# Setup of a two-layer graph kernel on one core: the score weights come in first, by column halves, and VectorE's setup work is reordered

## The chip, the cores and the metric

The kernel runs on one core of a Trainium2 chip. The metric is device time in microseconds (us) of one execution. Before the change three runs took 2207.53 us in the median (2207.39 to 2207.76).

A core has TensorE (PE, matrix products; PEld is its loading of weights), VectorE (DVE), ScalarE (ACT), GpSimd (POOL) and SyncE (SP), which here only issues transfers. Each takes its own instructions in the order in which they were built, and they wait for one another through semaphores. ACT and POOL issue transfers too. Transfers (DMAs) of all three run on the same 16 DMA engines: those of SP and ACT in two hardware queues, those of POOL in a software queue.

## The reference

128 graphs of 128 nodes with 512 features go through two layers. Cut to what matters:

```python
h = relu(layernorm(x))                         # layer 0
Xw = h @ Wv + bv
e  = leaky_relu((Xw @ aw[:d])[:, None, :] + (Xw @ aw[d:])[:, :, None] + ab, 0.2)
T  = adj * exp(e);  T = T / (T.sum(-1) + 1e-12)
x  = x + relu(h @ Wk[0] + T @ h @ Wk[1] + T @ T @ h @ Wk[2] + bk.sum(0))

h = relu(layernorm(x))                         # layer 1
q, k = split(h @ Wqk)
w  = mask / sqrt(512) * (q * (adj @ (k * mask))).sum(-1)
x  = x + softmax(w)[:, :, None] * (h @ Wv1)
```

All is fp32. `Wqk` is 512 x 1024 (2 MB), each `Wk[k]` and `Wv` is 512 x 512 (1 MB).

## The kernel before

**Algebra.** `Xw` is never formed: `Wv @ aw[:d]` and `Wv @ aw[d:]` are two columns (`attention_columns`, L252) that are put beside `Wk[2]` in the operand `r2` (`w` in the profile), so that one product of `h` gives `h Wk[2]` and both attention terms. `Wk[1]` and `Wk[0]` stand side by side in `r10` (`r` in the profile). For layer 1, the product of the two halves of `Wqk` is formed once (`score_matrix`, L316, the score matrix `M`, kept in `rl`), since `q . (adj k)` is a bilinear form of `h`.

**Products.** A product of `h` with 512 x 512 weights is done by `strassen` (L412): seven half-size products 1, 5, 6, 2, 7, 3, 4 in PSUM banks a, b, c, e, with sums of the left operand (`left_sums`, `sx`) and of the right one (`combine_steps`, L196: four subtractions on DVE, kept in `t2` for `r2` and in `t10` for `r10`; `t10` is `t` in the profile). The right operand of product 5 is the first subtraction, of 6 the second, of 7 the third, of 4 the fourth; products 1, 2 and 3 take plain blocks. `y2` (L487) is the product with `r2`, `y10` (L622) that with `r10`.

**Loops.** Graphs are taken in pairs. Layer 0 is a loop over 64 pairs (L809): `y10(p)`, `inner`, `outer`, `y2(p+2)`, `norm2`. Layer 1 is a loop over 32 groups of two pairs (L1157). All of this is unchanged.

**Setup (L762 to 805)** runs before the loop, and is what the change touches. Nothing may be reordered inside a chain that the code gives: `ordered` chains all products on PE, `behind("wk", ...)`, `behind("wq", ...)` and `tc.issue_after` put an instruction after a named one; within that, a planner chose the order of each engine when the program was built. The order on PE is:

1. `warm` and `warm_whole` (L226 to 237): products of ones that nobody reads, 7 small (128 columns), one of 512 columns, and later one of 512 and four small ones between the transposes;
2. 32 transposes of `Wqk` (`weights_transposed`, L301), one 128-row chunk after the other; ACT and DVE copy them out into `wqt` and `wkt`;
3. 8 transposes of the first pair's `h` and one of the node mask;
4. `score_matrix(f)` for f = 0 to 3, four products of 512 columns each;
5. `y2(0)`, whose first product needs `r2` with its attention columns, then `spread_columns(0)` and `y10(0)`, each of whose products needs `r10` or its combinations. The four products of 1 column between products 7 and 3 of `y2(0)` (`attention_constant`, L273) make a constant from `bv`, `aw` and `ab`, which DVE prepares in `constant_columns` (L266).

**Transfers.** SP issues `x` of pair 0, the four chunks of `Wqk` (512 KB each, rows of 4 KB), `x` of pair 1, then of each of `Wv` (`t` in the profile, it lies in the space of `t10`), `Wk[2]`, `Wk[1]` and `Wk[0]` the first two of four pieces. A piece (`rows`, L170) is 256 KB and goes to 32 partitions. POOL issues the other two pieces of each, after a small copy (`gate`, L178) that waits for the third chunk of `Wqk`; between those of `Wk[2]` and of `Wk[1]` it issues the three tiny loads `bvc`, `awc`, `ab_bc`, and after all of them the block-wise `adj` of pairs 0 and 1 (`agb`, L111).

Of the kernel before, what the change touches and what calls it, by code (L numbers as in the profile page):

```python
# [16 lines left out]
def kernel(  # L17
# [25 lines left out]
    nc = tc.nc  # L43
    B, N, D = x.shape
    K = wk.shape[0]
    P = 128
    DC = D // P
# [35 lines left out]
    def behind(what, op, *args, **how):  # L83

        with tc.issue_after(done[what]):
            return op(*args, **how)  # L86

    def ordered(op, *args, **how):

        with tc.issue_after(done["mm"]):  # L90
            done["mm"] = op(*args, **how).ins  # L91

    def bcast(ap, offset, n):

        return bass.AP(tensor=ap.tensor, offset=ap.offset + offset, ap=[[0, P], [1, n]])
# [45 lines left out]
    awc = setup.tile([P, 2, DC], FP, name="awc")  # L141
    bvc = setup.tile([P, DC], FP, name="bvc")

    load_x(0)
    for c in range(DC):
        nc.sync.dma_start(wqk_sb[:, c], wqk[c * P:(c + 1) * P])  # L146
    load_x(1)
    def blocks32(ap, offset, times, n):
        return bass.AP(tensor=ap.tensor, offset=ap.offset + offset, ap=[[0, times], [S32, n], [1, S32]])

# [19 lines left out]
    def rows(dst, w, chunks=range(DC), queue=nc.sync):  # L170

        for c in chunks:
            queue.dma_start(dst[c * S32:(c + 1) * S32],
                              w[c * P:(c + 1) * P].rearrange("(f a) o -> a f o", a=S32))


    gate = setup.tile([P, 1], FP, name="gate")
    done["gate"] = nc.gpsimd.tensor_copy(gate, wqk_sb[:, 2, :1]).ins  # L178
    weights0 = [(wv0_sb, wv0), (r2[:, :, 1:1 + D], wk[2])] + [(r10[:, :, k], wk[1 - k]) for k in range(2)]
    with tc.issue_after(done["gate"]):  # L180
        for dst, w in weights0[:2]:
            rows(dst, w, range(HC, DC), nc.gpsimd)
        nc.gpsimd.dma_start(bvc, bv0.rearrange("(p c) -> p c", c=DC))
        nc.gpsimd.dma_start(awc, aw.rearrange("(a p c) o -> p a (c o)", a=2, c=DC))
        nc.gpsimd.dma_start(ab_bc, bcast(ab, 0, 1))
        for dst, w in weights0[2:]:
            rows(dst, w, range(HC, DC), nc.gpsimd)
    for dst, w in weights0:
        rows(dst, w, range(HC))
    load_x(2)  # L190

# [34 lines left out]
    def warm_whole(bank):  # L226

        with tc.issue_after(done["mm"]):
            done["mm"] = nc.tensor.matmul(bank.rearrange("p (k n) -> p k n", n=P), ones,
                                          ones[:, None, :].to_broadcast([P, D // P, P]), start=True, stop=True).ins  # L230

    def warm(times, bank, start=True):

        for _ in range(times):
            with tc.issue_after(done["mm"]) if "mm" in done else ExitStack():
                done["mm"] = nc.tensor.matmul(bank[:, :P], ones, ones, start=start, stop=True,
                                              skip_group_check=True).ins
# [48 lines left out]
    def bias_columns():  # L286

        n = HD // S32
        v = bkt[:, 0, :2 * n]
        behind("wk", nc.vector.transpose, bkt.rearrange("p s j -> p (s j)"), bkj.rearrange("p s r -> p (s r)"))  # L290
        nc.vector.tensor_add(v, v, bkt[:, 0, 2 * n:])
        nc.vector.tensor_add(v, v, bkt[:, 1, :2 * n])
        done["wk"] = nc.vector.tensor_sub(v[:, n:], v[:, n:], v[:, :n]).ins

    def bias():

        n = HD // S32
        for i, to in enumerate((bias_a, bias_e)):
            behind("wk", over_partitions, to[:, 1], bkt[:, 0, i * n:(i + 1) * n], n)

    def weights_transposed(chunks):  # L301

        banks = [a2, e2, a1, b1, c1, e1]
        for c in chunks:
            for a in range(2):
                bank = banks[(c * 2 + a) % len(banks)]
                pt = bank.rearrange("p (o i) -> p o i", o=DC)
                for o in range(DC):
                    at = a * D + o * P
                    ordered(nc.tensor.transpose, pt[:, o, :], wqk_sb[:, c, at:at + P], ident)  # L310
                if a:
                    done["wk"] = behind("wq" if c == HC else "wk", nc.scalar.copy if c == HC else nc.vector.tensor_copy, wkt[:, :, c * P:(c + 1) * P], pt).ins
                else:
                    done["wq"] = behind("wq", nc.scalar.copy, wqt[:, :, :, c, :], pt.rearrange("p o (f a) -> p o f a", f=Q)).ins

    def score_matrix(f):  # L316

        bank = set1[f]
        for o in range(DC):
            ordered(nc.tensor.matmul, bank, wqt[:, o, f].rearrange("p c a -> p (c a)"), wkt[:, o],  # L320
                    start=(o == 0), stop=(o == DC - 1))
        done["m"] = done["mm"]
        nc.scalar.copy(rl[:, f, 0], bank)
# [68 lines left out]
    def transposed_by_pe(h, dst, banks):  # L392

        for j in range(G):
            pt = banks[j].rearrange("p (f n) -> p f n", f=Q)
            for f in range(Q):
                ordered(nc.tensor.transpose, pt[:, f, :], h[:, j, f * P:(f + 1) * P], ident)
            (nc.vector.tensor_copy if j else nc.scalar.copy)(dst[:, j], pt)

    def left_sums(hT):  # L400

# [357 lines left out]
                lambda: dve(nc.vector.tensor_sub, s[:, 3], b[0, 1], s[:, 1])]  # L759


    warm(7, e2)  # L762
    warm_whole(b2)
    done["warm"] = done["mm"]
    h0_rs = statistics(xg[0])
    done["wk"], done["wq"] = done["rs"], done["ln"]
    weights_transposed(range(1))
    h0 = behind("wq", norm_relu, xg[0], True, h0_rs)
    done["wq"] = done["h"]
    attention_vector_columns()  # L770
    attention_vector(0)
    warm_whole(c2)
    weights_transposed(range(1, 2))
    attention_vector(1)
    bias_columns()
    warm(2, b2, False)
    weights_transposed(range(2, 3))
    warm(2, b2, False)
    weights_transposed(range(3, 4))
    hT0 = lefts.tile([P, G, DC, N], FP, name="x")  # L780
    transposed_by_pe(h0, hT0, (a1, b1))
    masks()
    bias()
    rs1 = behind("wk", statistics, xg[1], "wq")
    LEFT[0] = left_sums(hT0)
    behind("left", attention_columns)
    for p in range(2):
        load_adj(p)
    for f in range(Q):
        score_matrix(f)  # L790
    behind("wq", norm0, 1, rs1)
    with tc.issue_after(done["u"]):
        right2 = combine(halves(r2, W2), [t2[:, i] for i in range(4)])
    constant_columns()
    with tc.issue_after(done["right"]):
        right10 = combine(halves(r10, HD), pairs(t10))
    with tc.issue_after(done["right"]), tc.issue_after(done["m"]):
        y2(0, {7: attention_constant})
        seed_a()
        seed_e()  # L800
        spread_columns(0)
        attention(0)
    with tc.issue_after(done["hv"]):
        load_x(3)
        load_adj(2)

    RS0 = {}

    for p in range(NP):  # L809
        weights, weights_end = [], None  # L810
# [622 lines left out]
```

## Time and profile before

| what | value |
|---|---|
| median of three runs | 2207.53 us |
| profiled execution, its own time | 2207.71 us |
| its span | 2205.9 us |
| PE busy | 2197.3 us (100% of the span) |
| DVE, ACT, POOL busy | 1699.8, 1233.0, 782.6 us |
| first product of `y2(0)` starts | 28.27 us |
| product 5 of `y10(0)` starts | 37.12 us |

The span is the time between the first and the last instruction of the core; 1.8 us of the execution's own time lie around it. PE is busy from 1.1 us on to the end, with 8.6 us of gaps in all, so a change in the setup is worth what it moves the work that PE can't skip. In the answers of the trace each line has a start and a length in us, then the engine, the source line, and what is written from what; in brackets stands the idle time before it and what ended it. A line number is often that of a helper, so the names of the tiles tell more.

### The profile page before, as it was taken

What the parts mean: (1) busy time and instruction counts of PE and PEld (TensorE: products, weight loads), DVE (VectorE), ACT (ScalarE), POOL (GpSimd) and SP (SyncE); (2) the same over time, 40 slices, a digit from 0 to 9 for tenths busy, and PEclk for the clock granted to TensorE, in tenths of its full rate; (3) what the DMA queues carried; (4) which work ended last, traced back from release to release, by engine and by line L of the source; (5) the groups of instructions that cost most, each with busy time, mean ns of one, the idle gap of its engine ahead of it and who ended that gap; (6) DMA issues with size and microseconds to landing.
All of it is one profiled execution on the core that took longest, in us unless ns stands there. A gap on an engine that the chain in (4) does not pass through costs nothing.

```text
span 2205.9 us, 29564 instructions
## 1 busy us (share of the span) xinstructions
PE 2197.3 (100%) x8127; PEld 1536.1 (70%) x8127; DVE 1699.8 (77%) x4544; ACT 1233.0 (56%) x2854; POOL 782.6 (35%) x957
## 2 busy tenths in 40 slices
PE   9999999999999999999999999999999999999998
PEld 6666666665666666566666666688788878887886
DVE  6778788777878877777877777588777777777777
ACT  4555555555555455555545554456666666666665
POOL 3222222222222222222222222255545554555454
PEclk9999999999999999999999999999999999999999
DMA  7788788887878888887878887867888788787877
GB/s 212 204 226 241 221 237 241 234 245 226 247 223 244 234 239 234 225 245 225 243 222 239 232 232 207 285 180 220 234 226 228 214 236 224 231 212 230 233 212 182
DMA packets 431874, 503.14 MB, mean 228 GB/s; under 512 B 102113, under 2 KB 280289, under 8 KB 427741
## 3 DMA queue, kind: packets, MB, share of 16 engines
q1 hardware_dynamic: 379544, 374.67, 56.1%
q0 software_dynamic: 51744, 126.05, 23.2%
q8 instruction: 65, 1.06, 0.2%
q14 instruction: 101, 0.82, 0.1%
q10 hardware_dynamic: 420, 0.54, 0.1%
HBM read 287.17 MB, written 213.94 MB: 227 GB/s over the span
## 4 chain that ended last, share of the span: by engine, by line
PE 98%; DMA 1%; DVE 1%; issue 0%; SPq 0%; DVEq 0%; POOL 0%
PE a L91 29%; PE c L91 26%; PE b L91 26%; PE e L91 17%; DMA t<-in_L_gnn_Wv_dram 0%; DMA tl<-in_L_gnn_Wqk_dram 0%; DVE junk L258 0%; DVE c L720 0%; DVE h L720 0%; DVE junk L720 0%; SPq L146 0%; DVEq L1429 0%; DVE x L389 0%; PE a L194 0%; SPq L101 0%
## 5 line engine op out<-in xcount | busy, mean ns | idle before, releaser
L720 POOL TENSOR_TENSOR c<-s,c 128x512 f32<-128x512 f32 (+1 forms) x186 | 201.2, 1095 | 252.3 <-DVE s L720 247.2
L475 POOL DMA_DIRECT2D fd<-fw x124 | 78.8, 639 | 492.8 <-DVE fw L463 458.5
L111 POOL DMA_DIRECT2D agb<-in_adj_dram x256 | 149.9, 592 | 260.2 <-DVE aT L86 235.5
L91 PE MATMUL a<-r,x 128*128 128x512 f32 x512 | 240.7, 592 | 0.0
L91 PE MATMUL b<-rw,in 128*128 128x256 f32 x884 | 212.0, 379 | 0.0
L91 PEld LDWEIGHTS b<-rw,in 128*128 128x128 f32 x884 | 168.0, 190 | 23.3 <-issue 0.5
L91 PEld LDWEIGHTS a<-r,x 128*128 128x128 f32 x512 | 97.1, 190 | 95.0 <-issue 91.3
L86 ACT COPY s<-c 128x257 f32<-128x257 f32 (+1 forms) x128 | 61.6, 481 | 171.4 <-PE c L91 171.4
L86 ACT COPY b<-a 128x257 f32<-128x257 f32 (+1 forms) x128 | 59.4, 464 | 167.7 <-PE a L91 165.2
L720 POOL TENSOR_TENSOR c<-c 128x1024 f32<-128x1024 f32 x61 | 144.2, 2363 | 10.9 <-DVE c L720 10.4
L91 PE MATMUL a<-w,x 128*128 128x257 f32 x512 | 132.0, 380 | 1.2 <-DVE w L86 1.1
L91 PE MATMUL b<-w,sx 128*128 128x257 f32 x512 | 132.1, 380 | 0.1
L463 DVE STREAM_TRANSPOSE fw<-hv 128x256 f32<-128x256 f32 x248 | 88.3, 414 | 52.1 <-DMA hv<-h2d 51.7
L91 PE MATMUL c<-t,sx 128*128 128x512 f32 x256 | 120.3, 592 | 0.0
L91 PE MATMUL e<-t,sx 128*128 128x512 f32 x256 | 120.3, 592 | 0.0
L91 PE MATMUL c<-t,x 128*128 128x512 f32 x256 | 120.3, 592 | 0.0
L91 PE MATMUL b<-t,sx 128*128 128x512 f32 x256 | 120.3, 592 | 0.0
L91 PE MATMUL b<-r,sx 128*128 128x512 f32 x256 | 120.3, 592 | 0.0
L720 DVE SCALAR_TENSOR_TENSOR junk<-agg,wscale,c 128x512 f32<-128x512 f32 x126 | 96.2, 763 | 30.0 <-POOL c L720 24.8
L720 ACT ACTIVATE c<-c,wcol 128x512 f32<-128x512 f32 x124 | 86.3, 720 | 55.7 <-DVE wcol L720 55.7
L86 ACT COPY c<-b 128x257 f32<-128x257 f32 (+1 forms) x128 | 59.4, 464 | 98.9 <-PE b L91 98.9
L91 PEld LDWEIGHTS a<-w,x 128*128 128x128 f32 x512 | 97.1, 190 | 15.9 <-DVE w L86 1.9
(282 smaller groups left out, 5318.3 us busy)
## 6 DMA issues: line engine op xcount, KB each, us to landing
fd<-fw POOLq DMA_DIRECT2D x93, 512.0 KB, 4.8
xg<-in_x_dram SPq DMA_DIRECT2D x64, 512.0 KB, 7.0
x1d<-x SPq DMA_DIRECT2D x64, 512.0 KB, 5.6
h2d<-h SPq DMA_DIRECT2D x64, 512.0 KB, 3.0
hd<-h SPq DMA_DIRECT2D x63, 512.0 KB, 3.1
hv<-hd SPq DMA_DIRECT2D x252, 128.0 KB, 3.9
hv<-h2d SPq DMA_DIRECT2D x248, 128.0 KB, 4.4
h<-h2d SPq DMA_DIRECT2D x62, 512.0 KB, 7.7
```

What stands on the lines that cost most here:

```text
L86: return op(*args, **how)
L91: done["mm"] = op(*args, **how).ins
L111: nc.gpsimd.dma_start(agb[p][c * S32:(c + 1) * S32].rearrange("p g q i -> p (g q) i"), v[c])
L463: done["c12"] = nc.vector.transpose(blocks[:, k, j].rearrange("p f (n b) -> p f n b", n=Q), hv[:, j].rearrange("p n (k f a) -> p k f n a", ...
L475: done["fd"] = nc.gpsimd.dma_start(FD[q].rearrange("p o j k n -> p o (j k n)")[:, slots], FW[0].rearrange("p o j k n -> p o (j k n)")[:, s ...
L720: done[engine] = op(*args, **how).ins
```

## The change

Six edits, all in the setup:

- `Wqk` is loaded in eight pieces of 256 KB (rows of 1 KB) in place of four of 512 KB: first the column half 0 of all chunks, then half 1. SP issues chunks 0 and 2, ACT chunks 1 and 3. `x` of pair 0 follows in SP's queue; it was first.
- All four pieces of `Wv` and of `Wk[2]` go into SP's queue, with `x` of pair 1 between the two. POOL's `gate` waits for `Wv`; after it POOL issues its two pieces of `Wk[1]` and of `Wk[0]`, then `bvc`, `awc`, `ab_bc`.
- The dummy products shrink to one small one and two of 512 columns, all at the start.
- `weights_transposed` takes a row half and a column half; `score_matrix` takes a column half, and each of the four sums is made of two parts, with the transposes of the next halves between them.
- On DVE, `attention_columns` come ahead of `left_sums`; the statistics of pair 1, the biases and the constant's columns move behind the combinations of `r2`; the four combinations of `r10`, which stood ahead of `y2(0)`'s additions, move behind them and into `attention(0)`.
- On ACT, both halves of pair 0's transposed `h` are copied (DVE copied one); the normalisation of pair 1 moves from ahead of `y2(0)` to behind its product 7.

The core of the diff:

```diff
+    for oh in range(2):
+        for ch in range(2):
+            for c in range(HC):
+                at = ch * HC + c
+                (nc.scalar if c else nc.sync).dma_start(
+                    wqk_sb[:, at].rearrange("p (a o) -> p a o", a=2)[:, :, oh * HD:(oh + 1) * HD],
+                    wqk[at * P:(at + 1) * P].rearrange("p (a o) -> p a o", a=2)[:, :, oh * HD:(oh + 1) * HD])
     load_x(0)
-    for c in range(DC):
-        nc.sync.dma_start(wqk_sb[:, c], wqk[c * P:(c + 1) * P])
-    load_x(1)
...
-    done["gate"] = nc.gpsimd.tensor_copy(gate, wqk_sb[:, 2, :1]).ins
     weights0 = [(wv0_sb, wv0), (r2[:, :, 1:1 + D], wk[2])] + [(r10[:, :, k], wk[1 - k]) for k in range(2)]
+    for dst, w in weights0[:2]:
+        rows(dst, w)
+        if dst is wv0_sb:
+            load_x(1)
+    done["gate"] = nc.gpsimd.tensor_copy(gate, wv0_sb[:, DC - 1, :1]).ins
     with tc.issue_after(done["gate"]):
-        for dst, w in weights0[:2]:
+        for dst, w in weights0[2:]:
             rows(dst, w, range(HC, DC), nc.gpsimd)
         nc.gpsimd.dma_start(bvc, bv0.rearrange("(p c) -> p c", c=DC))
         nc.gpsimd.dma_start(awc, aw.rearrange("(a p c) o -> p a (c o)", a=2, c=DC))
-        nc.gpsimd.dma_start(ab_bc, bcast(ab, 0, 1))
-        for dst, w in weights0[2:]:
-            rows(dst, w, range(HC, DC), nc.gpsimd)
-    for dst, w in weights0:
+        done["loads"] = nc.gpsimd.dma_start(ab_bc, bcast(ab, 0, 1)).ins
+    for dst, w in weights0[2:]:
         rows(dst, w, range(HC))
     load_x(2)
...
-    warm(7, e2)
+    warm(1, e2)
     warm_whole(b2)
-    done["warm"] = done["mm"]
-    h0_rs = statistics(xg[0])
...
+    warm_whole(c2)
+    done["warm"] = done["wk"] = done["wq"] = done["mm"]
+    weights_transposed(0, 0, (a2, e2))
+    weights_transposed(1, 0, (c1, e1))
+    attention_vector_columns()
+    attention_vector(0)
+    weights_transposed(0, 1, (a2, e2))
+    attention_vector(1)
+    score_matrix(0, 0)
+    masks()
+    score_matrix(1, 0)
+    h0_rs = behind("wk", statistics, xg[0], "wq")
+    behind("aggr", bias_columns)
+    weights_transposed(1, 1, (a2, e2))
+    score_matrix(2, 0)
+    score_matrix(3, 0)
     h0 = behind("wq", norm_relu, xg[0], True, h0_rs)
...
+    score_matrix(0, 1)
+    transposed_by_pe(h0, hT0, (a2, e2))
+    behind("wk", behind, "rs", attention_columns)
+    LEFT[0] = behind("u", left_sums, hT0)
+    for f in range(1, Q):
+        score_matrix(f, 1)
     for p in range(2):
-        load_adj(p)
...
+        behind("loads", load_adj, p)
     with tc.issue_after(done["u"]):
         right2 = combine(halves(r2, W2), [t2[:, i] for i in range(4)])
-    constant_columns()
-    with tc.issue_after(done["right"]):
-        right10 = combine(halves(r10, HD), pairs(t10))
-    with tc.issue_after(done["right"]), tc.issue_after(done["m"]):
-        y2(0, {7: attention_constant})
-        seed_a()
-        seed_e()
+    RS0 = {}
+
+    def beside_y2():
+
+        RS0[1] = behind("right", statistics, xg[1], "u2")
+        bias()
+        constant_columns()
+
+    right10_steps = combine_steps(halves(r10, HD), pairs(t10))
+    right10 = combined(halves(r10, HD), pairs(t10))
+    with tc.issue_after(done["m"]):
+        y2(0, {2: beside_y2, 7: attention_constant})
+        with tc.issue_after(done["right"]), tc.issue_after(done["rs"]):
+            for step in right10_steps[:2]:
+                step()
+        behind("u2", seed_a)
+        behind("s7", norm0, 1, RS0.pop(1))
+        behind("s7", seed_e)
         spread_columns(0)
         attention(0)
+        behind("lrelu", right10_steps[2])
+        behind("t", right10_steps[3])
```

More of the change, by code (lines that the diff above doesn't have):

```diff
@@ L298, in bias @@
         for i, to in enumerate((bias_a, bias_e)):
[L299 to L314, printed above, removed]
@@ L316, in score_matrix, with weights_transposed @@
-    def score_matrix(f):
+            behind("aggr", over_partitions, to[:, 1], bkt[:, 0, i * n:(i + 1) * n], n)
+    def weights_transposed(ch, oh, banks):
+        for a, bank in enumerate(banks):
+            pt = bank.rearrange("p (k n) -> p k n", n=P)
+            for c in range(HC):
+                for o in range(HC):
+                    at = a * D + (oh * HC + o) * P
+                    ordered(nc.tensor.transpose, pt[:, o * HC + c if a else c * HC + o, :],
+                            wqk_sb[:, ch * HC + c, at:at + P], ident)
+            if a:
+                on = "wq" if oh > ch else "wk"
+                done[on] = behind(on, nc.scalar.copy if oh > ch else nc.vector.tensor_copy,
+                                    wkt[:, oh * HC:(oh + 1) * HC, ch * HD:(ch + 1) * HD],
+                                    bank.rearrange("p (o n) -> p o n", o=HC)).ins
+            else:
+                done["wq"] = behind("wq", nc.scalar.copy,
+                                    wqt[:, oh * HC:(oh + 1) * HC].rearrange("p o f c a -> p (o f) c a")[
+                                        :, :, ch * HC:(ch + 1) * HC],
+                                    bank.rearrange("p (c o a) -> p o c a", c=HC, a=S32)).ins
@@ L318, in score_matrix @@
+    def score_matrix(f, oh):
         bank = set1[f]
-        for o in range(DC):
+        for o in range(oh * HC, (oh + 1) * HC):
             ordered(nc.tensor.matmul, bank, wqt[:, o, f].rearrange("p c a -> p (c a)"), wkt[:, o],
-                    start=(o == 0), stop=(o == DC - 1))
+                    start=(o == 0), stop=(o == DC - 1), skip_group_check=True)
         done["m"] = done["mm"]
-        nc.scalar.copy(rl[:, f, 0], bank)
+        if oh:
+            done["wq"] = behind("wq", nc.scalar.copy, rl[:, f, 0], bank).ins
@@ L397, in transposed_by_pe @@
                 ordered(nc.tensor.transpose, pt[:, f, :], h[:, j, f * P:(f + 1) * P], ident)
-            (nc.vector.tensor_copy if j else nc.scalar.copy)(dst[:, j], pt)
+            nc.scalar.copy(dst[:, j], pt)
     def left_sums(hT):
@@ L759, in inner_sums @@
                 lambda: dve(nc.vector.tensor_sub, s[:, 3], b[0, 1], s[:, 1])]
-    warm(7, e2)
+    warm(1, e2)
     warm_whole(b2)
-    done["warm"] = done["mm"]
-    h0_rs = statistics(xg[0])
-    done["wk"], done["wq"] = done["rs"], done["ln"]
-    weights_transposed(range(1))
+    warm_whole(c2)
[5 more added lines that the diff above has]
+    weights_transposed(0, 1, (a2, e2))
@@ L768 @@
+    attention_vector(1)
[7 more added lines that the diff above has]
+    score_matrix(3, 0)
     h0 = behind("wq", norm_relu, xg[0], True, h0_rs)
     done["wq"] = done["h"]
[L770 to L779, printed above, removed]
-    hT0 = lefts.tile([P, G, DC, N], FP, name="x")
[L781 to L786, printed above, removed]
+    score_matrix(0, 1)
+    hT0 = lefts.tile([P, G, DC, N], FP, name="x")
+    transposed_by_pe(h0, hT0, (a2, e2))
+    behind("wk", behind, "rs", attention_columns)
@@ L787 @@
+    LEFT[0] = behind("u", left_sums, hT0)
+    for f in range(1, Q):
+        score_matrix(f, 1)
     for p in range(2):
-        load_adj(p)
-    for f in range(Q):
-        score_matrix(f)
-    behind("wq", norm0, 1, rs1)
+        behind("loads", load_adj, p)
     with tc.issue_after(done["u"]):
         right2 = combine(halves(r2, W2), [t2[:, i] for i in range(4)])
-    constant_columns()
-    with tc.issue_after(done["right"]):
-        right10 = combine(halves(r10, HD), pairs(t10))
-    with tc.issue_after(done["right"]), tc.issue_after(done["m"]):
-        y2(0, {7: attention_constant})
-        seed_a()
-        seed_e()
+    RS0 = {}
@@ L805 @@
         load_adj(2)
-    RS0 = {}
     for p in range(NP):
```

## The prediction

> **What bounds the kernel now.** I read the page first, then the chain of waits of the first 120 us, then each engine's instructions in order up to 60 us, then the transfers in short stretches.
>
> ```profile
> span 2205.9 us, 29564 instructions
> PE 2197.3 (100%) x8127; PEld 1536.1 (70%) x8127; DVE 1699.8 (77%) x4544; ACT 1233.0 (56%) x2854; POOL 782.6 (35%) x957
> ```
>
> PE bounds the kernel: 8.6 us are idle in all. After the setup its work and order are the same in both kernels, so I compare one instant, product 5 of `y10(0)`, which I call X. What moves X moves the end. The chain of waits says what sets X today:
>
> ```profile
> 2.21 7.36 DMA tl<-in_L_gnn_Wqk_dram
> 9.75 9.44 DMA t<-in_L_gnn_Wv_dram
> 19.19 3.00 issue
> 22.19 0.70 DVE junk L258 x2
> ...
> 28.27 1.13 PE a L91 x4
> ```
>
> Third chunk of Wqk, POOL's half of Wv (complete at 22.2), the eight attention products `junk` on DVE, `y2(0)`. On PE, in order of time:
>
> ```profile
> 1.10 3.36 PE L236 MATMUL e<-ones 128*128 128x128 f32 x14 [1.10 <-DVE ones L161]
> 4.25 1.92 PE L229 MATMUL b<-ones 128*128 128x512 f32 x2
> ...
> 9.27 0.61 PE L236 MATMUL b<-ones 128*128 128x128 f32 x4
> ...
> 28.27 1.13 PE L91 MATMUL a<-w,x 128*128 128x257 f32 x4 [1.08 <-DVE w L86]
> ...
> 37.12 1.88 PE L91 MATMUL e<-t,sx 128*128 128x512 f32 x4
> ```
>
> So X = 37.12; PE was free for `y2(0)` at 27.2 (28.27 less the 1.08 in the bracket). The transfers set these times. First 11 to 16 us, where only SP's pieces of 32 partitions run; then 18 to 22 us, where SP's and POOL's run together; then two issues:
>
> ```profile
> DMA packets 535, 0.98 MB, mean 195 GB/s; under 512 B 59, under 2 KB 59, under 8 KB 535
> ```
> ```profile
> DMA packets 474, 1.21 MB, mean 303 GB/s; under 512 B 77, under 2 KB 77, under 8 KB 473
> ```
> ```profile
> bvc<-in_L_gnn_bv_dram POOLq DMA_DIRECT2D x1, 2.0 KB, 13.4
> awc<-in_L_gnn_aw_dram POOLq DMA_DIRECT2D x1, 4.0 KB, 13.3
> ```
>
> `awc`, issued at 12.56, lands at 25.9, right behind POOL's fourth piece (24.95), though it has 4 KB.
>
> [...]pieces 0 and 1 alone make 195 GB/s, beside pieces 2 and 3 together 303. [...]POOL's first large piece, issued at 9.75, moves its first bytes at 16.5, when the four pieces that SP issued before 6.2 are read. [...]a small dummy product takes 0.45 us at first (3.15/7), 0.22 at 9.27, and the step comes near 6.9.
>
> **The change, part by part.**
>
> *Dummy products.* Removed: 10 small (six at the start by 0.45 = 2.7 us, four later by 0.22 = 0.88); added none (two of 512 columns in both; one moves to half clock, +0.85). PE's own work shrinks by 2.7 us. This is the most that this edit can bring.
>
> *Wqk by halves.* Before, x and Wqk (2.6 MB) and 0.1 MB of small loads are read from 2.1 us on and have landed at 10.9; chunks 2 to 4 come 1.32 us apart, 400 GB/s. Rows of 1 KB are not in the trace; bounds are no loss (400) and the 310 GB/s of the stretch from 2 to 4 us. I take 340: all landed at 11.0 to 11.8, the parts that PE needs at 5.6, 7.4, 9.0 (half 0, half 1 of the upper chunks) and 11. PE then has from 9.9 the 16 products of 0.86 (13.7) and 17 transposes of 0.11: ready for `y2(0)` at 25.5[...]. Before: 27.2. Moving it to ACT's queue costs issue time only (0.44 each).
>
> *Wv and Wk[2] in SP's queue.* Now pieces 0, 1, 2, 3 of one weight follow one another[...]: 1.05 MB at 195 GB/s is 5.4 us. Wv is read from 10.0 to 15.4, landed 2.5 later (before, SP's first piece of w was read at about 15.2 and landed at 17.5, POOL's last at 22.05 and 24.95) at 17.9, against 22.2 before. x of pair 1 takes 1.4, Wk[2] 5.4: read at 22.1, landed at 24.6 (call it T0). The attention products end at 17.9 + 8 x 0.735 = 23.8, so Wk[2] is last. On DVE behind T0, from
>
> ```profile
> 27.95 0.29 DVE L86 COPY w<-ucol 128x4 f32<-128x4 f32 x2
> 28.27 2.63 DVE L199 TENSOR_TENSOR w<-w 128x514 f32<-128x514 f32 x4
> ```
>
> two copies 0.32, three left sums 0.99, the first combination 0.64: product 5 of `y2(0)` from T0 + 1.95 = 26.6. PE starts `y2(0)` near 26, so this much is a gain of about 2 us on 28.27.
>
> *The tiny loads, moved behind two more large pieces.* POOL's gate opens at 17.9, not 9.6, and `bvc`, `awc`, `ab_bc` stand behind all four pieces. By the order seen before, POOL's pieces are read after SP's that were issued over 3 us earlier (Wk[2], to 22.1), then share with SP's of Wk[1] and Wk[0]: 1.05 MB took 5.5 us (16.5 to 22.05) and 2.9 more to land: 30.5; `awc` 0.7 later, L = 31.2. DVE's first constant column waits for it. It is queued behind the combinations (T0 + 4.2) and pair 1's statistics (1.3), so it could start at T0 + 5.5 = 30.1: the load is late by 1.1.
>
> *What is queued behind it on DVE and ACT.* Pair 1's second aggregate, two bias transposes of 0.36, a wait for ACT's logarithm and exponential (0.6 after the aggregate, as at 15.76 to 16.36), second column and copy: the constant's products on PE can run at L + 1.5 = 32.7, while PE reaches them at about 26.5 + 5 x 0.87 = 30.9. Then pair 1's scale (four small ones, 0.8): L + 2.3. ACT stands waiting for it with `norm0(1)` (1.5), `seed_e` (0.55) and only then the copy of `y2(0)`'s last block, which the second `spread` needs:
>
> ```profile
> 27.90 0.59 ACT L607 COPY e<-bias_e 128x512 f32<-128x512 f32 x1
> ...
> 35.38 0.38 ACT L498 COPY y<-c 128x257 f32<-128x257 f32 x1 [1.80 <-PE c L91]
> ```
>
> Copy done at L + 4.75. In the new order of PE both spreads stand ahead of `y10(0)`; before, one product was between them. DVE reads the spread 0.41 later (as at 56.02 to 56.43), L + 5.15, and has, ahead of the first combination of `r10`:
>
> ```profile
> 34.75 2.48 DVE L199 TENSOR_TENSOR t<-r,t 128x1024 f32<-128x1024 f32 x2
> ...
> 38.07 0.73 DVE L86 TENSOR_SCALAR z<-a,y,cz 128x128 f32<-128x128 f32 x2
> 38.84 0.42 DVE L86 SCALAR_TENSOR_TENSOR z<-z 128x256 f32<-128x256 f32 x1
> 39.18 0.44 DVE L86 STREAM_TRANSPOSE aT<-agb 128x256 f32<-128x256 f32 x1
> ```
>
> 1.55 for these, 1.2 for the combination (2.48/2): X = L + 7.9. Before, these combinations were done at 37.15, beside `y2(0)`, for nothing; now they stand on the path. If `awc` isn't late, the same steps run from T0: X = T0 + 13.4 = 38.0.
>
> *The rest.* The third and fourth combinations end at X + 2.3 and X + 4.9; PE needs them at X + 5.4 and X + 8.8: free. ACT's second copy of `h` (0.6) is hidden by PE's score products; uncovered it costs 0.6. Pair 1 is stored about 9 us later than before (26.0), and its blocks are read at X + 9.4 on DVE, landed by 44: free, about 1 if the queue is full. `r10` and `agb` land by 33, used at 36 and 37.6.
>
> **Sum.** X = 31.2 + 7.9 = 39.1 against 37.12: +2.0 us. On the profiled execution's own 2207.7 (span 2205.9 and 1.8 around it) that is 2209.7; the median of the runs is 0.2 lower, so 2209.5. The edit gains 2 us at the start of `y2(0)` and gives back 4 by X.
>
> **Rivals.** 0.2% is 4.4 us, about what a measurement of this kernel can tell from no change.
>
> - *Gain kept.* Pieces 1 and 2 of a weight[...] overlap, and rows of 1 KB cost nothing: Wv at 16, T0 at 22, the tiny loads by 27. X = 22 + 13.4 = 35.4, 2205.8. For it: the landing times of before lag the reads, so there is slack. Against it: 195 GB/s held for all of 11 to 16 us. Over 4.4 us of gain needs X below 32.7, and so Wk[2] by 19.3, 5.2 MB at over 320 GB/s from 3 us on, which I all but exclude.
> - *Slower: POOL's pieces read last.* One mechanism: the software queue waits not only for Wk[2] but for SP's four pieces of Wk[1] and Wk[0] too, issued by 19. Read at 27.5, then POOL's alone at 195 GB/s to 32.9, landed 35.4, `awc` 36: X = 43.9, +6.8, 2214.3. It decides from L = 33.6 on. For it: 6.7 us from issue to first bytes before. Against it: SP's pieces issued at 8.31 to 10.9 then shared with POOL's.
> - *POOL shares at once.* Then Wk[2] lands at 26.8 and `awc` at 27.6: X = 26.8 + 13.4 = 40.2, +3.1, 2210.6.
> - *Nothing comes of it.* L at 29: X = 37 to 38, 2207.5 to 2208.4.
>
> **How the numbers follow.** Late by `awc` as summed 0.35, shared at once 0.15, nothing 0.12, gain kept 0.13, slower mechanism (or a clock halved again by PE's three waits, 1.9, 1.3 and 1.0 us) 0.25. Of the first two, 0.07 spill beyond 4.4; of the gain, 0.05. Faster 0.05, same 0.63, slower 0.32. The range leaves out the fastest and slowest tenth: 2205.6 to 2214.5.
>
> **What would show it.** Right: `y2(0)` begins near 26; the constant's products wait for DVE near 32.7; ACT's `y<-c` copy comes after `h<-xg`; e of `y10(0)` is released by DVE `t<-r` near 39. Wrong in the transfers: Wv complete before 16 or after 20, `awc` before 29 or after 34. Wrong altogether: X below 36, or PE gaps after 50 us that were not there.

## The result, and the profile after

The changed kernel takes 2212.52 us in the median of 11 runs (2210.82 to 2215.95); the kernel before, run beside it, 2207.55 (2205.85 to 2208.95). The ratio is 1.0025 with a 95% interval of 1.0017 to 1.0033: slower by 5.0 us, and clear of no change. The interval, 3.8 to 7.3 us, holds the 4.4 us (0.2%) at which the prediction put the border between "same" and "slower", so on which side of it the kernel lies is not settled. The profiled execution is itself the median one, 2212.52.

The head of the page of the changed kernel (busy time, share of the span, instructions):

```profile
span 2210.7 us, 29537 instructions
PE 2195.9 (99%) x8107; PEld 1533.0 (69%) x8107; DVE 1697.2 (77%) x4543; ACT 1231.9 (56%) x2855; POOL 779.1 (35%) x953
```

PE has 1.4 us less to do than before and 4.8 us more of span: 14.8 us of gaps in place of 8.6. The increase lies ahead of 46 us, where PE idles for 8.7 in place of 2.4. The chain of waits of the first 64 us of the changed kernel (start, length, what):

```profile
10.45 8.11 DMA t<-in_L_gnn_Wv_dram
...
18.71 0.18 POOL gate L187
...
19.25 2.26 POOL r L177 x4
...
22.05 11.94 DMA awc<-in_L_gnn_aw_dram
...
35.91 1.50 ACT h L369 x2
37.40 0.48 ACT e L619
37.88 0.31 ACT y L510
...
40.15 1.17 DVE t L205 x2
```

This is the chain of the prediction, link for link: the gate that now waits for `Wv`, four pieces of `r10`, then the 4 KB of `awc` that land 11.94 us after their issue, then DVE's first constant column and, queued behind it, pair 1's statistics on DVE and ACT (in the part left out), ACT's `h`, `e` and `y`, then the second spread and DVE's `z` (left out too), and at 40.15 the combination. On PE (timeline, with the idle time before each group and what ended it):

```profile
19.74 1.95 PE L91 MATMUL a<-wkt,wqt 128*128 128x512 f32 x4 [1.57 <-DVE wkt L86]
...
27.55 1.03 PE L91 MATMUL a<-w,x 128*128 128x257 f32 x4
...
35.25 0.61 PE L91 MATMUL c<-ccol,ones 128*128 128x1 f32 x4 [3.20 <-DVE r L353]
...
41.31 1.98 PE L91 MATMUL e<-t,sx 128*128 128x512 f32 x4 [0.69 <-DVE t L205]
43.67 1.96 PE L91 MATMUL b<-t,sx 128*128 128x512 f32 x4 [0.38 <-DVE t L205]
```

`y2(0)` begins 0.72 earlier than before (28.27), and X, product 5 of `y10(0)`, 4.19 later (37.12). Product 6 follows 2.36 after X where it was 1.72: 0.64 more. It needs the second combination of `r10`, and DVE made the third ahead of that. In these lines `t<-r` is the first or the third, which read `r10` alone, and `t<-r,t` the second or the fourth (DVE, timeline):

```profile
40.07 2.31 DVE L205 TENSOR_TENSOR t<-r 128x1024 f32<-128x1024 f32 x2
42.31 1.22 DVE L205 TENSOR_TENSOR t<-r,t 128x1024 f32<-128x1024 f32 x1
```

The first product of `inner(0)` is 4.91 later (PE of the kernel before, then of the changed one):

```profile
47.64 0.59 PE L91 MATMUL a<-y,tt 128*128 128x256 f32 x2
```
```profile
52.55 0.59 PE L91 MATMUL a<-y,tt 128*128 128x256 f32 x2
```

So X makes 4.19 of these 4.91 and product 6 another 0.64. From there on both kernels are alike: in all the profiled executions of this document the time is that instant plus 2159.8 to 2160.1 us. So a run's time less 2160.0 tells when its setup was done, and the spread of the runs is a spread of the setup.

The 3.20 us are the wait for `awc`, which DVE takes up at 34.02. Behind the 1.57 us stands another load, `awj` (DVE, timeline):

```profile
14.42 0.21 DVE L86 STREAM_TRANSPOSE awt<-awj 128x32 f32<-128x32 f32 x1 [5.31 <-DMA awj<-in_L_gnn_aw_dram]
...
34.02 0.16 DVE L86 SCALAR_TENSOR_TENSOR awc<-awc,bvc 128x4 f32<-128x4 f32 x1 [2.50 <-DMA awc<-in_L_gnn_aw_dram]
```

`awj` had no wait before (its transpose ran at 8.23); now ACT issues it at 7.26, behind its four pieces of `Wqk`, and the statistics and the copy of `wkt` are queued behind its transpose. From 12 to 16 us, where SP's large pieces run alone, the transfers move 205 GB/s.

### The profile page after: what moved, and what is told of

The parts are those of the page before. It is cut to its first block, busy times and chain, and to the rows that moved or that the text cites. A ratio compares the mean times of both kernels' runs of the same rounds, so it can differ in the third digit from the quotient of the medians.

```text
span 2210.7 us, 29537 instructions
## 1 busy us (share of the span) xinstructions
PE 2195.9 (99%) x8107; PEld 1533.0 (69%) x8107; DVE 1697.2 (77%) x4543; ACT 1231.9 (56%) x2855; POOL 779.1 (35%) x953
## 4 chain that ended last, share of the span: by engine, by line
PE 97%; DMA 1%; DVE 1%; issue 0%; ACT 0%; POOL 0%; SPq 0%; DVEq 0%; POOLq 0%
PE a L91 28%; PE c L91 26%; PE b L91 26%; PE e L91 17%; DMA awc<-in_L_gnn_aw_dram 1%; DMA t<-in_L_gnn_Wv_dram 0%; DMA tl<-in_L_gnn_Wqk_dram 0%; DVE c L732 0%; DVE t L205 0%; POOL r L177 0%; DVE h L732 0%; SPq L148 0%; ACT h L369 0%; DVE z L86 0%; DVE junk L732 0%
## 5 line engine op out<-in xcount | busy, mean ns | idle before, releaser
L732 DVE SCALAR_TENSOR_TENSOR junk<-agg,wscale,c 128x512 f32<-128x512 f32 x126 | 96.1, 763 | 29.8 <-POOL c L732 24.6
L91 PE MATMUL a<-rw,f 128*128 128x256 f32 x448 | 108.1, 379 | 0.0
```

The lines of the kernel that those rows point to most:

```text
L732: done[engine] = op(*args, **how).ins
```

## The experiments

Theory A: the late `awc` sets X, and the rest of the loss is what the chain behind it costs. Rivals: the new order on VectorE and ScalarE would make the loss without `awc` (B); TensorE's waits halve its clock (C), the other half of the prediction's slower case; the transfers in one queue are the cause (D). All kernels are the changed one but for the edit shown, or the kernel before where the label says so. The medians come from 5 to 21 runs each; ratios are against the kernel before on the same chip.

| label | median us | ratio, 95% interval | awc used | X | inner(0) | profiled run's time |
|---|---|---|---|---|---|---|
| before | 2207.55 | | 30.83 | 37.12 | 47.64 | 2207.71 |
| changed | 2212.52 | 1.0025, 1.0017 to 1.0033 | 34.02 | 41.31 | 52.55 | 2212.52 |
| tiny_first | 2213.67 | 1.0029, 1.0018 to 1.0040 | early | 38.48 | 50.95 | 2210.94 |
| no_wait_for_awc | 2210.64 | 1.0017, 1.0009 to 1.0026 | not at all | 39.31 | 51.51 | 2211.46 |
| combinations_first | 2211.24 | 1.0020, 1.0010 to 1.0030 | 33.89 | 41.44 | 51.96 | 2211.93 |
| pieces_0213 | 2211.38 | 1.0019, 1.0009 to 1.0028 | 32.79 | 41.65 | 52.89 | 2212.86 |
| awj_first | 2214.31 | 1.0029, 1.0017 to 1.0041 | 33.50 | 43.04 | 54.28 | 2214.31 |
| waits_filled | 2210.50 | 1.0015, 1.0008 to 1.0021 | 32.86 | 39.86 | 50.49 | 2210.47 |
| before_late_loads | 2206.95 | 0.9997, 0.9989 to 1.0006 | 30.32 | 35.52 | 46.05 | 2206.08 |
| all_mended | 2208.27 | 1.0006, 1.0000 to 1.0013 | early | 42.28 | 54.65 | 2214.68 |
| dummies_back | 2213.83 | 1.0032, 1.0021 to 1.0044 | 33.11 | 40.41 | 52.87 | 2212.86 |
| before_fewer_dummies | 2207.46 | 1.0002, 0.9994 to 1.0011 | in time | 37.73 | 48.25 | 2208.28 |
| mended_dummies | 2209.19 | 1.0008, 1.0000 to 1.0016 | early | 35.97 | 47.73 | 2207.80 |
| mended_two_queues | 2210.06 | 1.0019, 1.0010 to 1.0027 | early | 42.83 | 53.35 | 2213.16 |

"Early" and "in time" mean that DVE did not wait for `awc`. A profile is one run out of a spread of some 2 to 8 us. So for a wait's place and size I read the profile, for what an edit is worth the median and its interval; where two intervals overlap, as those of most of the variants do with the changed kernel's, the difference of the medians is not clear of the spread.

### tiny_first: the tiny loads at the start

```diff
+    nc.gpsimd.dma_start(bvc, ...)      # behind bkj, ahead of the gate
+    nc.gpsimd.dma_start(awc, ...)
+    nc.gpsimd.dma_start(ab_bc, ...)
...
-        nc.gpsimd.dma_start(bvc, ...)
-        nc.gpsimd.dma_start(awc, ...)
-        done["loads"] = nc.gpsimd.dma_start(ab_bc, ...).ins
+        done["loads"] = done["row"]
```

> The changed kernel with bvc, awc and ab_bc issued by GpSimd at the very start, right behind its small loads of bk, and nothing else moved (adj still waits for the last large piece). If the late awc sets product 5 of y10(0) (X, 41.31 in the changed kernel): VectorE's wait of 2.50 us for awc disappears, the constant's products run near 32.8 and not 35.25, ScalarE's copy of y2(0)'s last block ends near 35.7, X is 38.6 to 39.6, and the time falls by 2 to 2.7 us, to about 2210. If instead the new order on VectorE and ScalarE is itself the cause and awc only hides it (rival): X stays at 40.5 or later and the time within 1 us of the changed kernel's 2212.5.

X came at 38.48, 2.83 earlier, and there was no wait for `awc`; B's 40.5 or later is out. But B has a part: X is still 1.36 later than in the kernel before, with nothing waiting for `awc`, since the normalisation of pair 1 on ACT and `z` on DVE stand ahead of it in the new order. And in the same run 1.2 us were lost again before `inner(0)`. On PE and ACT (timeline):

```profile
45.69 1.98 PE L91 MATMUL c<-t,sx 128*128 128x512 f32 x4 [0.96 <-ACT c L86]
```
```profile
44.62 0.30 ACT L86 ACTIVATE r<-mv,eps 128x2 f32<-128x2 f32 x1 [3.48 <-DVE mv L345]
...
45.06 0.58 ACT L86 COPY c<-b 128x512 f32<-128x512 f32 x1
```

ACT stands at the logarithm of the next pair's statistics, which on DVE are queued behind the fourth combination, and the copy that product 7 needs stands behind it. The planner made this order; in the changed kernel ACT had that copy first. The median of the seven runs did not fall (2210.94 to 2217.41). Why the other six are so much later than the profiled one is not shown: no profile of them exists. Two of them have a mean granted clock of 0.998, which fits C; the 0.999 of the others is found in the kernel before too.

### no_wait_for_awc: the wait taken away, the transfers kept

```diff
-                   awc[:, a], awc[:, a], 1.0, bvc, ...
+                   zeros[:, :DC], zeros[:, :DC], 1.0, zeros[:, DC:], ...
-    ... nc.vector.tensor_copy, c1[:, D - 1:], ab_bc)
+    ... nc.vector.tensor_copy, c1[:, D - 1:], zeros[:, :1])
```

> The changed kernel with its transfers untouched, but the constant's two columns and ab are made from a tile of zeros, so the output lacks the constant of the attention and nobody reads bvc, awc and ab_bc; VectorE has one small memset more. It takes the wait away without moving a transfer. If the wait is the cause: X 38.6 to 39.6, as with the loads put first, and the time 2 to 2.7 us lower; the two runs agree within 0.5 us in X. If taking three small loads from behind the large pieces changes the landing of the pieces themselves (rival for the run with the loads first), only that one gains.

X came at 39.31, 2.00 earlier, and the median is 1.9 us below the changed kernel's, just short of A's 2 to 2.7. The chain behind `awc` was indeed gone, ACT's copy of `y` started at 33.87 and not 37.83, but then another load was late. DVE (timeline):

```profile
37.70 0.45 DVE L86 STREAM_TRANSPOSE aT<-agb 128x256 f32<-128x256 f32 x1 [1.85 <-DMA agb<-in_adj_dram]
```

The block transpose of `adj` waits for `agb`, which POOL issues last of all, and the first combination of `r10` stands behind it, at 38.07. Less these 1.85 us X would have been near 37.5 (an estimate, 39.31 - 1.85). In the changed kernel the same late load is covered by the later `awc`. Behind X half of the gain is gone again: PE had waited 2.63 us, and product 5 took 3.56 us in place of 1.98, at a granted clock of 0.51 from 39.4 to 42.6. `inner(0)` is 1.04 earlier.

### combinations_first: two combinations ahead of z

```diff
-        attention(0)
+        with tc.issue_after(done["right"]):
+            attention(0)
```

> The changed kernel with attention(0) asked for behind the first two combinations of r10, so that VectorE makes these two ahead of z, leaky ReLU and the block transpose of adj (1.55 us), as soon as y2(0)'s additions are done at 37.3. awc stays late. If the combinations behind z are the last link of the path, as the prediction has it: first combination done near 38.5, second near 39.7; X follows product 1 of y10(0) without a gap, 40.4 (0.9 us earlier), product 6 has no wait for VectorE (0.38 less); time 1.0 to 1.5 us lower. Rival: z and with it the exponential come 2.4 us later, and inner(0) waits for the transposed attention, so that what X gains is given back by 52.6: time unchanged or up to 1 us higher.

Product 5 follows product 1 without a gap, and product 6 doesn't wait. The median is 1.3 us lower, as A said, though not clear of the spread, and `inner(0)` had no wait for the attention. X itself was at 41.44, not 40.4, since in this run product 4 of `y2(0)` took 1.62 (1.03 in the changed kernel) and product 1 of `y10(0)` 2.55 (1.96): behind the wait of 2.97 us for the constant the granted clock was 0.50 from 36.9 to 40.1.

### pieces_0213: the pieces in another order

```diff
-        rows(dst, w)
+        rows(dst, w, (0, 2, 1, 3))
```

> The changed kernel with SyncE's four pieces of Wv and of Wk[2] issued in the order 0, 2, 1, 3 in place of 0, 1, 2, 3, so that neighbours in the queue go to different halves of the partitions. If [...]the queue overlaps neighbours: the stretch from 12 to 16 us moves near 300 GB/s in place of about 190, Wv is complete near 16.5 to 17 and not 18.6, Wk[2] near 23.5 to 24.5 and not 26.2, awc lands at 32 to 33, X is 39.3 to 40.3, time 1 to 2 us lower. y2(0) itself can start no earlier than 27.5, when the score products end. If a queue works through its pieces one by one whatever their partitions (rival): the same times within 0.3 us.

D in the form of this run's expectation, that neighbours in the queue on the same half of the partitions cost a third of the rate, is refuted. From 12 to 16 us the transfers moved 226 GB/s against 205 in the changed kernel (204 to 211 in the other variants with its order of pieces), 10% more and far from 300; with the order 0, 2, 1, 3 mended_dummies has 225, all_mended 185. The prediction's own stretch with both queues allows another reading (kernel before, 18 to 22 us; queue, packets, MB, share; q0 is POOL's, q1 SP's):

```profile
q0 software_dynamic: 236, 0.77, 65.1%
q1 hardware_dynamic: 237, 0.43, 38.4%
```

A packet of POOL's held 3.3 KB and one of SP's 1.8 KB, while the packets per us rose only from 107 (SP's alone, 535 in 5 us) to 118 (474 in 4 us). So most of the step from 195 to 303 goes with the larger packets of POOL's queue. That they are its cause no run shows.

`Wk[2]` and `awc` came about a microsecond earlier (DVE doesn't wait for `Wk[2]` any more, `awc` is used at 32.79), which waits_filled, whose transfers are the changed kernel's, has too. And yet X was at 41.65. Here the clock is in view. Windows of the timeline: stretch, its length, PE busy and instructions, granted clock, DMA share, GB/s:

```profile
31.30:34.70 3.40, 1.45 (x9) 1.00 1.08 249
34.70:38.00 3.30, 3.30 (x9) 0.50 0.46 142
```

After a wait of 1.95 us for the constant, the clock was 0.50 for some 3.3 us. Products 3 and 4 of `y2(0)` took 1.91 and 1.92 in place of 1.11 and 1.03, and what the earlier `awc` had gained was gone.

### awj_first: the attention vector's load ahead

```diff
-    nc.scalar.dma_start(awj, blocks32(aw, 0, Q, S32))
+    nc.gpsimd.dma_start(awj, blocks32(aw, 0, Q, S32))
```

> The changed kernel with awj, the small load of the attention vector, in GpSimd's queue ahead of its other small loads; in the changed kernel ScalarE issues it behind its four pieces of Wqk. Everything else as in the changed kernel. Theory: awj lands near 9 to 10 and not 14.4, VectorE's wait of 5.3 us for it is gone, the statistics and the copy of wkt that are queued behind it come 1 to 1.6 us earlier, TensorE's wait of 1.57 us ahead of the second part of the score sums falls below 0.3, and the score products end near 26.1 in place of 27.55. But awc still lands near 34, so that the constant's products stay near 35.2 and X near 41.3: the time is within 0.5 us of the changed kernel's, since only the wait for awc grows, by about 1 us. Rival: if the wait for awj sets the end, X falls by 1.4 us with it.

Both waits for `awj`, 5.31 on DVE and 1.57 on PE, are gone, and the score products end at 26.44. The order of the waits was right, the time was not: 2214.31 where no change was expected, though with five runs the interval covers the changed kernel's. In the profile X was 1.7 later. The wait for the constant had grown from 3.20 to 3.63, and a stretch of halved clock followed, twice as long as the one above:

```profile
30.00:33.30 3.30, 1.11 (x6) 1.00 1.11 246
33.30:40.00 6.70, 5.01 (x14) 0.50 0.61 170
```

Four of its five runs have a mean clock of 0.998 or less, three of eleven for the changed kernel. Taking away a wait that hid under another one made the other longer. In this profile the slow stretch behind it is what cost; that it is so in the median five runs don't show.

### waits_filled: dummy products in the wait

```diff
+        for _ in range(3):
+            ordered(nc.tensor.matmul, b1..., ones, ones..., start=True, stop=True)
         attention_constant()
```

> The changed kernel with three dummy products of 512 columns (0.86 us each, 2.6 us) on TensorE between product 7 of y2(0) and the constant's products, where TensorE waits 3.2 us for awc's users. The wait itself stays. Theory: the spread of the changed kernel's runs (2210.8 to 2216.0, where the kernel before has 2205.9 to 2208.9) is the clock, which is halved [...](seen in the profiles of three of the experiments at 0.50, after waits of 2 to 3 us); each such stretch costs 1.7 us. Then no granted clock below 1 between 34 and 44 us, the profiled X near 41.3, the highest run 1 to 2 us lower than 2216 and the median 0.3 to 1.2 us lower. Rival: the spread has another cause (transfers that land at other times): median and spread unchanged, or later by up to 0.3 where the dummies outlast the wait.

The dummies ran from 31.23 to 33.97, and the constant's products followed at 34.09:

```profile
34.09 0.61 PE L91 MATMUL c<-ccol,ones 128*128 128x1 f32 x4
```

The median fell by 2.0 us and the highest of 21 runs is 2213.33; one of the 21 has a clock of 0.998. The narrower spread fits C. The median is not shown to be C's. The changed kernel's median run, which is its profiled one, has no halved clock to lose, and the two profiles differ by 2.06 at `inner(0)` for other reasons. `awc` was used 1.16 earlier, at 32.86, which nothing in the edit explains. The rest comes from DVE, where the planner, with the dummies on PE, chose another order (timeline):

```profile
38.58 1.23 DVE L205 TENSOR_TENSOR t<-r 128x1024 f32<-128x1024 f32 x1
39.72 0.44 DVE L86 STREAM_TRANSPOSE aT<-agb 128x256 f32<-128x256 f32 x1
40.08 1.18 DVE L205 TENSOR_TENSOR t<-r,t 128x1024 f32<-128x1024 f32 x1
```

The first combination stands ahead of the transpose of `adj`, and X is 7.00 behind `awc` in place of 7.29; the second stands ahead of the third, product 6 doesn't wait, and 0.61 more are gained. So the run does not separate the filled wait from the new order.

### before_late_loads: the late place in the old order

```diff
         for dst, w in weights0[2:]:
             rows(dst, w, range(HC, DC), nc.gpsimd)
+        nc.gpsimd.dma_start(bvc, ...)
+        nc.gpsimd.dma_start(awc, ...)
+        nc.gpsimd.dma_start(ab_bc, ...)
```

> The kernel before with bvc, awc and ab_bc behind GpSimd's four pieces of r10, and nothing else: the place that the change gives them, in the old order of VectorE, where the four combinations of r10 stand ahead of y2(0)'s additions and ScalarE's normalisation of pair 1 ahead of y2(0). The constant's columns stand ahead of these combinations. awc lands near 33 to 34 (the pieces have landed by 32.5). If the late load alone makes the loss: the constant's products move from 33.0 to about 34.5, the four combinations of r10 (4.9 us) start at 34 and not at 32.5, X moves to 38.5 to 40.5, 1.5 to 3.5 us more than 2207.3. If it is harmless without the new order on VectorE and ScalarE (rival): X within 0.5 us of 37.12.

The rival is right: no loss, 0.9997. DVE waits, but little stands behind the wait (timeline):

```profile
30.32 0.16 DVE L86 SCALAR_TENSOR_TENSOR awc<-awc,bvc 128x4 f32<-128x4 f32 x1 [1.59 <-DMA awc<-in_L_gnn_aw_dram]
```

The combinations of `r10` begin at 30.97, the constant's products ran without a gap at 31.51, and X was 8.61 behind the start of `y2(0)`, before 8.85. With the old gate `awc` comes at 30.3 and not 34, so this shows that with the old gate and the old order the place in the queue is harmless; the loss needs the later gate, the new order, or both. What 34 would cost in the old order was not run.

### all_mended: every named loss taken out

```diff
+    make_identity(nc, ident)           # first on POOL, then all small loads, awj too
...
+        rows(dst, w, (0, 2, 1, 3))
...
+    bias()                             # and the two constant columns, behind bias_columns
...
-        behind("s7", norm0, 1, RS0.pop(1))
         behind("s7", seed_e)
+        behind("y10", norm0, 1, RS0.pop(1))
...
+        with tc.issue_after(done["right"]):
+            attention(0)
```

> The changed kernel with each loss taken out: GpSimd makes the identity first and then issues awj, nm, bk, bvc, awc and ab_bc; SyncE's pieces in the order 0, 2, 1, 3; the biases and the constant's columns on VectorE ahead of the attention products; the combinations of r10 ahead of z; ScalarE's seed_e and last copy of y2(0) ahead of the normalisation of pair 1. If these are all that the change loses, y2(0) starts at 26 to 26.6, its last copy ends near 34.5, X follows product 1 of y10(0) at 36.3 to 37, and the time is 2206.7 to 2207.5, within 0.5 us of the kernel before or just below it; the earlier start of y2(0), some 2 us, can't be kept in full, since r10 lands at 33.6 and the combinations with it. Rival: something not named here still waits, X above 38, time above 2208.5.

2208.27 in the median: 4.25 of the 4.97 us are back, and the ratio to the kernel before is 1.0006, 0.7 us (the interval allows 0 to 2.9). Together the named losses are nearly all there is, though which of the edits brought how much, and what the 0.7 are, stays open. The profiled run was the latest of the 21, 2214.68. It shows the clock once more, here at the start, after a wait of 2.60 for `Wqk`:

```profile
5.80:9.10 3.30, 0.70 (x7) 1.00 0.98 295
9.10:15.90 6.80, 6.13 (x19) 0.50 1.09 228
```

So X at 42.28 in the table belongs to that run and not to the median one.

### dummies_back and before_fewer_dummies: the dummy products alone

```diff
     weights_transposed(0, 0, (a2, e2))
+    warm(2, b2, False)
     weights_transposed(1, 0, (c1, e1))
+    warm_whole(c2)
```

> The changed kernel with dummy products put back where TensorE waits for Wqk: two small ones behind the first two blocks of transposes, one of 512 columns behind the next two (1.1 us in all at full clock), and nothing else. Theory: the removed dummy products were no gain, since TensorE only waits in their place, and in some runs these waits (0.5 and 0.8 us in the profile of the changed kernel, 2.6 us in a slow run of all_mended) halve the clock in the score products[...]; then the profile is the same as the changed kernel's within 0.3 us at y2(0)'s start and X, and the median falls by 0.3 to 1 us, the highest runs by 1 to 2. Rival: the dummies stand in the way of the transposes: y2(0) later by 0.3 to 1 us; X, which awc sets, and the median unchanged or up to 0.3 higher.

The median is not lower, and the profile shows something that neither theory had: the planner, with two steps more on PE, put ACT's logarithm of the first statistics ahead of its copy of `maskT`. The logarithm waits for DVE and so for `awj`, and the third score product for that copy:

```profile
17.43 1.98 PE L91 MATMUL c<-wkt,wqt 128*128 128x512 f32 x4 [2.98 <-ACT maskT L289]
```

`y2(0)` began at 28.71. It says nothing on the dummy products, but shows `awj` on the path where ACT's order doesn't cover it. The other direction is clean:

```diff
-    warm(7, e2)
+    warm(1, e2)
     warm_whole(b2)
+    warm_whole(c2)
...
-    warm_whole(c2)                     # between the transposes
-    warm(2, b2, False)                 # twice, between the transposes
```

> The kernel before with the change's dummy products alone: one small one and two of 512 columns at the start, none between the transposes. Wv and the attention products set y2(0) there, so that TensorE's 2.7 us of saved work only turn into waits: y2(0) within 0.3 us of 28.3 (or of 26.9, where Wv lands earlier), X with it, the median within 0.5 us of 2207.5. Rival: the clock is halved in the transposes or the score products, which then end after 27: X and the median 0.5 to 2 us later, with a granted clock of 0.5 in the profile or a wider spread.

In the kernel before the dummy products are worth nothing: 1.0002, and no clock below 1 in the profile, though PE waits up to 1.44 for `Wqk`. The 2.7 us that they took off PE became waits.

### mended_dummies and mended_two_queues

```diff
+    warm(2, b2, False)                 # on all_mended, as in dummies_back
+    warm_whole(c2)
```

> all_mended with the same three dummy products put back. Theory: its slowest runs (2214.5 and 2214.7, the one that was profiled among them, with a clock of 0.50 from 9 to 16 us after a wait of 2.6 us for Wqk) come from the clock in the transposes and first score products: median 0.3 to 0.8 us below 2208.27, highest run below 2212. What bounds X then is GpSimd's share of r10, near 35 to 36: X 36.5 to 38, and the time 2207 to 2208. Rival: Wqk itself lands late in those runs and the dummies change nothing: median within 0.3 us, slow runs above 2213 still there.

The median is 2209.19, not below all_mended's: the dummies don't pay here either. The highest run is 2212.88, so the latest runs are gone, but with 13 runs that may be chance. The profiled run is worth a look, since X is at 35.97, 1.15 ahead of the kernel before. PE, then ACT (timeline):

```profile
38.83 1.98 PE L91 MATMUL b<-t,sx 128*128 128x512 f32 x4 [0.97 <-ACT b L86]
```
```profile
37.24 0.42 ACT L86 ACTIVATE z<-z 128x256 f32<-128x256 f32 x1 [2.12 <-DVE z L86]
...
38.20 0.57 ACT L86 COPY b<-a 128x512 f32<-128x512 f32 x1
```

With the combinations first, `z` is later, ACT waits for it, and the copy that product 6 needs is queued behind. The gain is given back within one product: `inner(0)` at 47.73, before 47.64.

```diff
-        rows(dst, w, (0, 2, 1, 3))
+        rows(dst, w, range(HC))
...
-    done["gate"] = ... wv0_sb[:, DC - 1, :1]
+    done["gate"] = ... wqk_sb[:, 2, :1]
+        for dst, w in weights0[:2]:
+            rows(dst, w, range(HC, DC), nc.gpsimd)
```

> mended_dummies with the transfer edit undone: pieces 2 and 3 of Wv and of Wk[2] go back to GpSimd's queue, and its gate opens with the first half of Wqk's third chunk (near 6 us). Theory: two queues at once move about 300 GB/s where SyncE's alone moves about 200, so Wv is complete at 16 to 19, Wk[2] at 22 to 25, r10 before 32 and adj by 36; y2(0) starts at 26 to 26.5, bound by the score products, X is 35.5 to 36.5, and the time 2206 to 2207.2, faster than the kernel before by 0.3 to 1.5 us. Rival: GpSimd's pieces are read only after SyncE's and share with Wk[2]: Wv or Wk[2] complete after 25, X above 37, the time as mended_dummies or above.

The rival is right: the ratio is above all_mended's and mended_dummies', so putting these pieces back into two queues, with the gate open early, brings nothing. In the profiled run `Wqk` too was late, beside POOL's pieces (PE waits 1.91 for it at 9.42, and the clock is 0.50 from 9.8 to 13.1). Two queues did move more, 269 GB/s from 12 to 16 us against 225 in mended_dummies, but in the wrong order. POOL's pieces of `r10` had landed by 27.6, while the piece of `Wk[2]` that is needed first was still out (DVE, timeline):

```profile
32.08 0.24 DVE L86 COPY w<-ucol 128x4 f32<-128x4 f32 x2 [2.43 <-DMA w<-in_L_gnn_Wk_dram]
```

On PE this wait is the last 0.70 only. The score products had ended as late as 31.5, after the 1.91, the slow stretch, and 1.96 more for ACT's copy of `maskT`, as in dummies_back.

## Why the prediction was right, and where it was wrong

The time, 2212.5, lies within the range, and the likeliest case had the right mechanism, but 3.0 us too small. That put the median 0.6 beyond the 4.4 us up to which the prediction called the kernel the same. The sum of the difference at X: `awc` 2.8 later, the chain behind it 0.6 shorter, so X at 41.3 and not 39.1. Behind X come some 0.7 that the prediction did not have.

- *Chain behind awc.* Predicted X = L + 7.9, with L the landing of `awc`; measured 7.29 in the changed kernel, and 7.00 and 7.30 in waits_filled and dummies_back. Where the clock was halved on the way it was 7.55, 8.86 and 9.54 (combinations_first, pieces_0213, awj_first). That `awc` sets X is shown: no_wait_for_awc and tiny_first, which take the wait away in two ways, bring X 2.0 and 2.8 forward. The other 1.4 of the 4.2 at X remain without the wait for `awc` (tiny_first); they belong to the new order, for which the prediction had X = T0 + 13.4.
- *When awc lands.* This is the term that was mis-sized: L = 34.0, not 31.2, past the 33.6 from which the prediction itself has the kernel slower. `Wk[2]` landed at 26.2, not 24.6, and POOL's pieces, issued from 19.25 on, moved their first bytes near 25.8, when SP's pieces of `Wk[2]` were read, and not at 22.1. The last of them landed at 33.6, not 30.5, and `awc` right behind it. L was 32.8 to 34.0 over six profiles, so the changed kernel's profile is at the late end. The slower rival's own mechanism, POOL's pieces read last, is not seen: they landed from 28.7 on, side by side with SP's.
- *Moving it to ACT's queue costs issue time only.* Wrong. `awj` stands behind the four pieces on ACT, landed at 14.4, and its queue on DVE reached PE: the score products ended at 27.55, not 25.5, and the gain at `y2(0)` is 0.7 and not 2. That this left the sum standing is luck: in the changed kernel it is hidden by `awc` again (awj_first: no gain).
- *Third and fourth combination free.* The fourth is. The third was made ahead of the second, and product 6, which needs the second, waits for it, 0.64 after X. In waits_filled, where the second comes first, it doesn't wait.
- *`r10` and `agb` land by 33.* Wrong by up to 5: `agb` at 37.7 in no_wait_for_awc and near 38.0 in the changed kernel (issued at 31.56, landed 6.4 later), covered there by the later `awc`, which is luck again.
- *Clock halved again.* It was put into the slower case with waits of 1.9, 1.3 and 1.0 us. In the changed kernel's profile, its median run, the clock is never halved, though the largest wait is 3.20, for the constant. In the profiles of six variants it is (0.50, after waits of 1.91 to 3.63), so it has a part in the spread; how large a part, and whether any in the median, is not settled. The half clock of the first dummy products in the prediction is read from their times alone, 0.45 us against 0.22 later; the granted clock in the profile of the kernel before is 1.00 there too, from 1.0 to 7.0 us.
- *195 GB/s alone, 303 beside.* The rate of SP's queue was as predicted (205). Why it is higher beside POOL's was not shown: with SP's queue alone, alternating the halves of the partitions brought 10% (226), and the packets of POOL's queue are larger (3.3 KB against 1.8). And with two queues the gain in rate (269 against 225) brought no time.

## What to carry to other kernels

Ask of each load, however small, what stands ahead of it in its queue and what is queued behind its first reader: the same tiny loads at the end of POOL's queue cost nothing in the old order, where they came at 30.3, and some 2 us at X in the new one, where a later gate brought them at 34.0. Take the next waits into account before crediting the removal of one; here `awj`, `agb` and a copy on ACT each stood right behind. Look at the order in which a planner puts the steps of one engine after each edit: a third combination ahead of the second cost 0.64, and an edit on TensorE alone changed that order. And a wait of TensorE may cost more than its length: in six of fourteen profiles the granted clock was 0.50 for the products after one of 1.91 to 3.63 us, though others of up to 3.20 left it at 1.00. Whether dummy products in the wait itself pay is open; elsewhere in the setup they brought nothing.

## What was not expected of the hardware

The granted clock went to 0.50 after waits of 1.91 (mended_two_queues), 1.95 (pieces_0213), 2.60 (all_mended), 2.63 (no_wait_for_awc), 2.97 (combinations_first) and 3.63 us (awj_first), and stayed there for 3.2 to 3.3 us, in all_mended and awj_first for twice that (6.8, 6.7), while 3.20 us in the changed kernel, 2.98 in dummies_back and 1.96 in mended_two_queues left it at 1.00. PE had not been idle throughout ahead of it: in the 3.3 or 3.4 us before, it had been busy for 0.70 us (all_mended) to 1.78 (combinations_first). Why a wait does it in some runs and not in others, no run shows.

In the setup POOL's ninth transfer was not issued until one of the eight ahead of it had landed. In the changed kernel four pieces of `r10`, three tiny loads and one piece of `agb` are issued by 23.9, and the next `agb` waits 4.83 us for a piece of `r10`; in the kernel before, the ninth behind the gate waits 5.07 us for a piece of `Wv`. So `agb` is late by more than its own bytes. Whether the chip sets this limit or the semaphores that this program uses for its transfers, no run shows.
